# Triangle's two layer norms: variances of four chunks side by side, scale spread by a second product

## The chip, the core and the metric

The kernel runs on one core of a Trainium2 chip. Its time is the device time of one execution in microseconds (us); the figure compared is the median over repeated runs. A profile is one further execution, recorded instruction by instruction. The engines named below are PE (TensorE, matrix products into PSUM), DVE (VectorE), ACT (ScalarE), POOL (GpSimd) and SP (SyncE, which here only issues DMAs). "PEld" is PE loading a stationary operand.

## The reference

Four layers work one after another on an image of 256 by 256 pixels with 128 channels, each preceded by a group norm and added to its input: attention, a gated recurrence, a triangle multiplication and a convolution. The change touches the third. Its core:

```python
def layer_norm(x, w, b):
    mu = jnp.mean(x, axis=-1, keepdims=True)
    var = jnp.var(x, axis=-1, keepdims=True)
    return (x - mu) * jax.lax.rsqrt(var + EPS) * w + b

pair_norm = layer_norm(pair, ln_in_w, ln_in_b)           # first norm
p = jnp.einsum('bijd,hd->bijh', pair_norm, p_in_w)
g = jax.nn.sigmoid(jnp.einsum('bijd,hd->bijh', pair_norm, g_in_w))
left  = g[..., :H] * p[..., :H]
right = g[..., H:] * p[..., H:]
out = jnp.einsum('bikd,bjkd->bijd', left, right / jnp.float32(L))
out = layer_norm(out, ln_out_w, ln_out_b)                # second norm
out = jnp.einsum('bijh,dh->bijd', out, p_out_w)
gate = jax.nn.sigmoid(jnp.einsum('bijd,ed->bije', pair_norm, g_out_w))
return gate * out
```

Both norms run over the 128 channels, which lie on the 128 partitions. So mean and variance of a pixel are sums over partitions, and the kernel forms them with matrix products.

## The kernel before

`triangle` works on the image as [128 channels, 65536 pixels] in three stages. All PE, ACT and DVE instructions of the first and third stage are pinned: each engine runs them in the order in which the code issues them.

**Stage 1, the first norm** (L999 to L1034) walks over 64 blocks of 1024 pixels, two of them to a DMA of 1 MB. For one block, `centre` multiplies the input by a centring matrix `lc` (two products of 512 columns into the PSUM tile `zc`) and ACT squares it into `sq`. `normalise` multiplies `sq` by `omat`, a 128 by 128 matrix of 1/128, so that every partition of `var` holds the variance of its pixel; ACT makes `rs` from it by Ln and Exp, DVE multiplies `zc` by `rs` and then applies the norm's weight and bias, both on DVE. `centre` of block b+1 is issued ahead of `normalise` of block b. `zc` has three PSUM buffers of two banks, `var` one. After each second block POOL's queue writes `zn` to DRAM (`znT`).

**Stage 2** (L1036 to L1068) reads `znT` four times and forms the gated products and the sum over k. It is not touched.

**Stage 3** (L1074 to L1160) walks over 32 pairs of blocks. In the order of PE's products for pair p: `var` (from `sq` of p, four products), `pe` (output gate, four), `zc` of pair p+1 (four), `py` (output product, four). ACT makes `rs` twice, loads the sigmoid table, makes `ga` from `pe` twice, squares `zc` twice and loads the table for Ln and Exp again. DVE multiplies `zc` by `rs` into `on`, then gates, adds the residual and collects statistics. `zc` has two PSUM buffers; `var`, `pe` and `py` share two more under the tag "z". Three loads of 1 MB and one store of 1 MB go with each pair.

A PSUM tile's buffer is given to the next tile of the same tag when every reader of the old tile is done. The stage that matters here is therefore set by three things: the in-order queues of PE, ACT and DVE, the number of buffers of a tag, and what reads a tile last.

A float32 product of 128 by 512 shows up as two LDWEIGHTS and two MATMUL records. In the attention stage (L306 to L350) the same kind of norm is done for the first layer: there DVE copies the centred tile to SBUF as `zs` (L318 to L324), POOL applies weight and bias (L336), and a small product `pbias` (L338) puts four chunks side by side in the array.

Of the kernel before, what the change touches and what calls it, by code (L numbers as in the profile page):

```python
# [17 lines left out]
P = 128  # L18
# [12 lines left out]
class Kernel:  # L31
# [21 lines left out]
    def act(self, out, in_, func, bias=0.0, scale=1.0, **kw):  # L53
        return self.nc.scalar.activation(out, in_, func, bias=bias, scale=scale, **kw)  # L54
# [4 lines left out]
    def mm(self, out, lhsT, rhs, start=True, stop=True):  # L59
        return self.nc.tensor.matmul(out, lhsT, rhs, start=start, stop=stop)  # L60
# [898 lines left out]
    def triangle(self, x2T, x3T, znT, prodD, stats2, shift2, stats3, prepare):  # L959
# [3 lines left out]
        nc, tc, I = self.nc, self.tc, self.i  # L963
        V = nc.vector
        NB, G, CQ = NPIX // 1024, 4, P // 4
        pin = lambda f: lambda *a, **k: tc.keep_in_program_order(f(*a, **k))  # L966
        mm, act, copy = pin(self.mm), pin(self.act), pin(nc.scalar.copy)
        tt, ts, stt, bn = pin(V.tensor_tensor), pin(V.tensor_scalar), pin(V.scalar_tensor_tensor), pin(V.bn_stats)
        table = pin(nc.scalar.preload_act_table_set)
        flat = lambda t: t.rearrange("p k n -> p (k n)")  # L970
        MUL, ADD = ALU.mult, ALU.add
        with ExitStack() as c:
# [17 lines left out]
                        V.tensor_copy(wf[:, :, 2 * n + side, :],  # L990
                                      wpg[m][:, side * P:(side + 1) * P].rearrange("c (g d) -> c g d", g=G))

            zs = c.enter_context(ExitStack())
            zp = zs.enter_context(self.pool(name="tz", bufs=5))


            with ExitStack() as c1:
                io = c1.enter_context(self.pool(name="t1", bufs=3))
                work = c1.enter_context(self.pool(name="t1w", bufs=2))  # L999
                ps = c1.enter_context(self.pool(name="t1s", bufs=3, space=PSUM))  # L1000
                xin, zn, zc, sq = {}, {}, {}, {}

                def centre(b):
                    if b >= NB:
                        return
                    if b % 2 == 0:
                        xin[b // 2] = io.tile([P, 2048], F32, name="xin")
                        nc.sync.dma_start(xin[b // 2], x2T[:, b * 1024:(b + 2) * 1024])
                        zn[b // 2] = io.tile([P, 2048], F32, name="zn")
                    zc[b] = ps.tile([P, 2, 512], F32, name="zc")  # L1010
                    for k in range(2):
                        s = (b % 2) * 1024 + k * 512
                        mm(zc[b][:, k], lc, xin[b // 2][:, s:s + 512])
                    sq[b] = work.tile([P, 1024], F32, name="sq")
                    act(sq[b], flat(zc[b]), AF.Square, bias=cb)

                def normalise(b):
                    var = ps.tile([P, 2, 512], F32, name="var", bufs=1)
                    for k in range(2):
                        mm(var[:, k], self.omat, sq[b][:, k * 512:(k + 1) * 512])  # L1020
                    rs = work.tile([P, 1024], F32, name="rs")
                    act(rs, flat(var), AF.Ln, bias=self.eps)
                    act(rs, rs, AF.Exp, scale=-0.5)
                    z = zn[b // 2][:, (b % 2) * 1024:(b % 2 + 1) * 1024]
                    stt(z, flat(zc[b]), cb, rs, ADD, MUL)
                    ts(z, z, lnw, lnb, MUL, ADD)
                    if b % 2 == 1:
                        nc.gpsimd.dma_start(znT[:, (b - 1) * 1024:(b + 1) * 1024], zn[b // 2])

                table(LN_EXP)  # L1030
                centre(0)
                for b in range(NB):
                    centre(b + 1)
                    normalise(b)  # L1034

            with ExitStack() as c1:  # L1036

# [29 lines left out]
                        nc.gpsimd.dma_start(prodD[g * CQ + d].rearrange("(p a j) -> p a j", p=P, a=2),  # L1067
                                            o.rearrange("p a j b -> p a (j b)"))  # L1068

            zs.close()  # L1070
            prepare(W["kt"], W["wd"], W["bv"])


            with ExitStack() as c1:  # L1074
                io = c1.enter_context(self.pool(name="t3", bufs=3))
                work = c1.enter_context(self.pool(name="t3w", bufs=3))
                ps = c1.enter_context(self.pool(name="t3s", bufs=2, space=PSUM))
                D = [{} for _ in range(NB // 2)]

                def product(wt, src, h, name, **kw):  # L1080
                    z = ps.tile([P, 2, 512], F32, name=name, **kw)
                    for k in range(2):
                        mm(z[:, k], wt, src[:, h * 1024 + k * 512:h * 1024 + (k + 1) * 512])
                    return flat(z)

                def load(p):
                    if p < NB // 2:

                        for n, src in (("zn", znT), ("pr", prodD), ("xin", x2T)):
                            t = D[p][n] = io.tile([P, 2048], F32, name=n)  # L1090
                            for c0, c1 in ((0, 96), (96, P)) if n == "pr" and p == 0 else ((0, P),):
                                nc.sync.dma_start(t[c0:c1], src[c0:c1, p * 2048:(p + 1) * 2048])

                def centre(p):
                    if p < NB // 2:
                        d = D[p]
                        d["zc"] = [product(self.cmat, d["pr"], h, "zc") for h in range(2)]
                        d["sq"] = []
                        for h in range(2):
                            sq = work.tile([P, 1024], F32, name="sq")  # L1100
                            act(sq, d["zc"][h], AF.Square)
                            d["sq"].append(sq)

                def stats(h):
                    for k in range(2):
                        o = h * 1024 + k * 512
                        bn(stats3[:, 4 * p + 2 * h + k, :], x3[:, o:o + 512])

                def gates(p):
                    pe = [product(we, D[p]["zn"], h, "pe", tag="z") for h in range(2)]  # L1110
# [12 lines left out]
                table(LN_EXP)  # L1123
                for p in range(NB // 2):
                    d = D[p]
                    load(p + 2)
                    on, py, x3 = [], [], io.tile([P, 2048], F32, name="x3")
                    hs = [slice(h * 1024, (h + 1) * 1024) for h in range(2)]
                    var = [product(self.omat, d["sq"][h], 0, "var", tag="z") for h in range(2)]
                    for h in range(2):  # L1130
                        rs = work.tile([P, 1024], F32, name="rs")
                        act(rs, var[h], AF.Ln, bias=self.eps)
                        act(rs, rs, AF.Exp, scale=-0.5)
                        on.append(work.tile([P, 1024], F32, name="on"))
                        tt(on[h], d["zc"][h], rs, MUL)
                    if p:
                        gates(p)
                    ga = d["ga"]
                    centre(p + 1)
                    if p + 1 < NB // 2:  # L1140
                        table(LN_EXP)
                    py = [product(wo, on[h], 0, "py", tag="z") for h in range(2)]
# [291 lines left out]
```

## Time and profile before

| what | value |
|---|---|
| runs | 5235.69 us median of 3 (5234.29 to 5239.15) |
| profiled execution | 5238.88 us, span 5237.0 us |
| DVE busy over the span | 4091.4 us (78%) |
| ACT busy over the span | 3684.9 us (70%) |
| POOL busy over the span | 344.4 us (7%) |
| stage 1, first `zc` product to first product of stage 2 | 3284.57 to 3525.38 us |
| stage 3, first `pe` product to start of the last store | 4228.02 to 4700.49 us |

The span is the stretch from the first to the last instruction of the profiled execution; its own time is 1.9 us longer. Busy shares over the whole span mix four layers with different limits, so the two stages are read by themselves, from the timeline of their steady part and from busy times in a window. Stage 1 repeats with every pair of blocks, stage 3 with every pair too, and each has 32 of them.

### The profile page before, as it was taken

To read this page: it belongs to the slowest core of one execution; us is meant where nothing else is said; L and a number is where in the kernel's file an instruction comes from. 1 tells how busy PE (TensorE), PEld (TensorE's weight loads), DVE (VectorE), ACT (ScalarE), POOL (GpSimd) and SP (SyncE) were. 2 spreads that over 40 slices of the span, in tenths; PEclk is the share of its full clock that TensorE was granted. 3 is DMA by queue.
4 is the path that set the end of the run, shared out by engine and by line. 5 is a ranking of instruction groups with operands and counts; after the bars stand their busy time and mean duration, and the time that the engine had idled before them with its cause. 6 is when DMAs were issued, how large, how long until landed. Compare 5 with 4: busy or idle time off the path is not lost.

```text
span 5237.0 us, 75959 instructions
## 1 busy us (share of the span) xinstructions
PE 4997.8 (95%) x30067; PEld 2805.6 (54%) x30067; DVE 4091.4 (78%) x4886; ACT 3684.9 (70%) x5051; POOL 344.4 (7%) x552
## 2 busy tenths in 40 slices
PE   6699999999999899999999998999999989989999
PEld 4433555555555333333333333349999944339999
DVE  5665999999999799999999999554433446679886
ACT  4376888888888799999999998883333357762110
POOL 1132000000000000000000000000011000000000
PEclk7799999999999899999999999999999999999999
DMA  8875222222222122122222221767766678855432
GB/s 290 335 271 206 73 86 82 85 80 83 86 85 82 62 70 70 66 73 68 70 70 67 73 70 65 286 253 272 251 229 231 224 288 295 295 206 188 148 123 65
DMA packets 185921, 788.58 MB, mean 151 GB/s; under 512 B 36083, under 2 KB 39432, under 8 KB 136384
## 3 DMA queue, kind: packets, MB, share of 16 engines
q1 hardware_dynamic: 120212, 514.73, 29.2%
q0 software_dynamic: 60416, 268.46, 13.3%
q8 instruction: 240, 3.93, 0.3%
q10 hardware_dynamic: 4936, 0.50, 0.1%
q14 instruction: 117, 0.96, 0.1%
HBM read 512.28 MB, written 271.32 MB: 150 GB/s over the span
## 4 chain that ended last, share of the span: by engine, by line
issue 50%; PE 41%; DVE 5%; POOL 2%; DMA 1%; ACT 1%; POOLq 0%; ACTq 0%; DVEq 0%; SPq 0%
PE z L60 9%; PE m L60 7%; PE zc L60 4%; PE po L60 4%; PE nd L60 3%; PE sc L60 3%; PE var L60 2%; PE py L60 2%; DVE stats L966 1%; DVE x L966 1%; PE ppq L60 1%; PE ppv L60 1%; PE px L60 1%; PE ppk L60 1%; PE ppg L60 1%
## 5 line engine op out<-in xcount | busy, mean ns | idle before, releaser
L471 DVE TENSOR_TENSOR e<-sc,bT 128x1024 f32<-128x1024 f32 x512 | 602.9, 1219 | 52.0 <-PE sc L60 52.0
L54 ACT ACTIVATE e<-e 128x1024 f32<-128x1024 f32 x512 | 540.3, 1055 | 64.1 <-DVE e L471 54.9
L966 DVE TENSOR_TENSOR LR<-z,sg 128x512 f32<-128x512 f32 x256 | 268.3, 1049 | 365.6 <-ACT sg L54 358.6
L60 PE MATMUL m<-U,v 128*128 128x128 f32 x4608 | 516.6, 276 | 6.6 <-DVE v L1281 6.6
L60 PEld LDWEIGHTS m<-U,v 128*128 128x128 f32 x4608 | 516.4, 192 | 6.7 <-DVE v L1281 6.7
L60 PE MATMUL z<-wf,zt 128*128 128x128 f32 x4096 | 460.9, 276 | 4.3 <-DVE zn L966 3.6
L60 PEld LDWEIGHTS z<-wf,zt 128*128 128x128 f32 x4096 | 460.6, 193 | 5.5 <-DVE zn L966 4.4
L54 ACT ACTIVATE sg<-z 128x512 f32<-128x512 f32 x256 | 152.8, 597 | 308.7 <-PE z L60 306.8
L60 PE MATMUL var<-sq,omat 128*128 128x512 f32 x768 | 360.8, 599 | 1.2 <-ACT rs L54 1.2
L54 ACT ACTIVATE rs<-var,eps 128x1024 f32<-128x1024 f32 x192 | 213.2, 1111 | 169.7 <-PE var L60 169.7
L60 PE MATMUL sc<-tq,tk 32*128 32x256 f32 x4096 | 299.0, 403 | 2.3 <-DVE e L471 1.4
L471 DVE TENSOR_TENSOR ks<-e 128x1024 f32<-128x1024 f32 x256 | 300.6, 1215 | 0.0
L60 PEld LDWEIGHTS sc<-tq,tk 32*128 32x128 f32 x4096 | 187.6, 185 | 160.3 <-issue 97.1
L60 PE MATMUL nd<-e,tv 128*32 128x256 f32 x4096 | 271.8, 383 | 0.0
L60 PE MATMUL zc<-xin,lc 128*128 128x512 f32 x512 | 248.6, 609 | 6.0 <-DVE zn L966 5.5
L54 ACT ACTIVATE dn<-dn 128x512 f32<-128x512 f32 x384 | 241.6, 629 | 12.7 <-DVE dn L471 1.9
L60 PEld LDWEIGHTS var<-sq,omat 128*128 128x128 f32 x768 | 137.9, 189 | 203.8 <-issue 155.2
L60 PE MATMUL av<-y,ident 128*128 128x512 f32 x384 | 192.2, 609 | 44.0 <-DVE y L803 44.0
L60 PE MATMUL po<-LR 128*128 128x256 f32 x1024 | 222.2, 380 | 6.9 <-DVE LR L966 6.9
L1318 ACT COPY m4s<-m 128x512 f32<-128x512 f32 x32 | 18.7, 585 | 286.8 <-PE m L60 286.8
L60 PEld LDWEIGHTS po<-LR 128*128 128x128 f32 x1024 | 194.1, 190 | 34.2 <-DVE LR L966 7.7
L54 ACT ACTIVATE rs<-rs 128x1024 f32<-128x1024 f32 x192 | 202.9, 1057 | 6.1
(325 smaller groups left out, 10085.5 us busy)
## 6 DMA issues: line engine op xcount, KB each, us to landing
zt<-znT SPq DMA_DIRECT2D x128, 1024.0 KB
znT<-zn POOLq DMA_DIRECT2D x64, 1024.0 KB, 4.7
xin<-x2T SPq DMA_DIRECT2D x64, 1024.0 KB
xr<-x3T SPq DMA_DIRECT2D x46, 768.0 KB
xin<-in_x_dram SPq DMA_DIRECT2D x64, 512.0 KB
xT<-xo POOLq DMA_DIRECT2D x64, 512.0 KB, 10.5
xr<-xT SPq DMA_DIRECT2D x64, 512.0 KB
xin<-xT SPq DMA_DIRECT2D x32, 1024.0 KB
```

What stands on the lines that cost most here:

```text
L54: return self.nc.scalar.activation(out, in_, func, bias=bias, scale=scale, **kw)
L60: return self.nc.tensor.matmul(out, lhsT, rhs, start=start, stop=stop)
L471: pin = lambda f: lambda *a, **k: tc.keep_in_program_order(f(*a, **k))
L966: pin = lambda f: lambda *a, **k: tc.keep_in_program_order(f(*a, **k))
L1318: nc.scalar.copy(m4, m[4])
```

## The change

For a pair of blocks there are now four chunks of 512 pixels. A product with `m32`, a [128, 32] matrix of 1/128, gives the variance of one chunk on 32 partitions; four such products write the four quarters of one [128, 512] tile `var`. Ln and Exp then run once over [128, 512] for the pair, in place of twice over [128, 1024]. A second product, with `spread` (all 1/32) over the 32 partitions of a chunk, spreads the scale to 128 partitions: `pr`, two PSUM tiles of [128, 1024]. Since `pr` lies in PSUM, the centred tile is first copied to SBUF as `zs`: by DVE in stage 1 (which adds the bias `cb` on the way), by ACT in stage 3. DVE multiplies `zs` by `pr`. In stage 1, weight and bias are applied by POOL.

All [128, 1024] PSUM tiles of a stage now share one tag, "w", with three buffers of two banks; `var` has the tag "r" with two buffers of one bank.

```diff
+            m32 = wp.tile([P, 32], F32, name="tmean")
+            V.memset(m32, 1.0 / P)
+            spread = wp.tile([P, P], F32, name="tspread")
+            V.memset(spread, 1.0 / 32)
+
+            def variance(ps, work, sq):
+                var = ps.tile([P, 512], F32, name="var", tag="r", bufs=2)
+                for k in range(4):
+                    mm(var[32 * k:32 * k + 32], m32, sq[k // 2][:, (k % 2) * 512:(k % 2 + 1) * 512])
+                rs = work.tile([P, 512], F32, name="rs")
+                act(rs, var, AF.Ln, bias=self.eps)
+                act(rs, rs, AF.Exp, scale=-0.5)
+                return rs
+
+            def spreads(ps, rs):
+                pr = [ps.tile([P, 1024], F32, name="pr", tag="w") for _ in range(2)]
+                for k in range(4):
+                    mm(pr[k // 2][:, (k % 2) * 512:(k % 2 + 1) * 512], spread[32 * k:32 * k + 32], rs[32 * k:32 * k + 32])
+                return pr
...
-                work = c1.enter_context(self.pool(name="t1w", bufs=2))
+                work = c1.enter_context(self.pool(name="t1w", bufs=4))
...
-                    act(sq[b], flat(zc[b]), AF.Square, bias=cb)
+                    act(sq[m, b], zc, AF.Square, bias=cb)
+                    zs[m, b] = work.tile([P, 1024], F32, name="zs")
+                    add(zs[m, b], zc, cb)
...
-                centre(0)
-                for b in range(NB):
-                    centre(b + 1)
-                    normalise(b)
+                for m in range(2):
+                    load(m)
+                centre(0, 0)
+                centre(0, 1)
+                for m in range(NB // 2):
+                    load(m + 2)
+                    centre(m + 1, 0)
+                    rs = variance(ps, work, [sq[m, b] for b in range(2)])
+                    centre(m + 1, 1)
+                    pr = spreads(ps, rs)
+                    zn = io.tile([P, 2048], F32, name="zn")
+                    for b in range(2):
+                        z = zn[:, b * 1024:(b + 1) * 1024]
+                        tt(z, zs[m, b], pr[b], MUL)
+                        nc.gpsimd.tensor_scalar(z, z, lnw, lnb, MUL, ADD)
+                    nc.gpsimd.dma_start(znT[:, m * 2048:(m + 1) * 2048], zn)
...
-                ps = c1.enter_context(self.pool(name="t3s", bufs=2, space=PSUM))
+                ps = c1.enter_context(self.pool(name="t3s", bufs=3, space=PSUM))
...
-                        d["zc"] = [product(self.cmat, d["pr"], h, "zc") for h in range(2)]
-                        d["sq"] = []
+                        d["zs"], d["sq"] = [], []
                         for h in range(2):
+                            zc = product(self.cmat, d["pr"], h, "zc")
                             sq = work.tile([P, 1024], F32, name="sq")
-                            act(sq, d["zc"][h], AF.Square)
+                            act(sq, zc, AF.Square)
                             d["sq"].append(sq)
+                            z = work.tile([P, 1024], F32, name="zs")
+                            act(z, zc, AF.Copy)
+                            d["zs"].append(z)
...
-                    var = [product(self.omat, d["sq"][h], 0, "var", tag="z") for h in range(2)]
-                    for h in range(2):
-                        rs = work.tile([P, 1024], F32, name="rs")
-                        act(rs, var[h], AF.Ln, bias=self.eps)
-                        act(rs, rs, AF.Exp, scale=-0.5)
-                        on.append(work.tile([P, 1024], F32, name="on"))
-                        tt(on[h], d["zc"][h], rs, MUL)
+                    rs = variance(ps, work, d["sq"])
                     if p:
                         gates(p)
+                    pr = spreads(ps, rs)
+                    for h in range(2):
+                        on.append(work.tile([P, 1024], F32, name="on"))
+                        tt(on[h], d["zs"][h], pr[h], MUL)
```

The order of PE's products is then, for a pair in stage 1: `zc` (first half of the next pair), `var`, `zc` (second half), `pr`. In stage 3: `var`, `pe`, `pr`, `zc` of the next pair, `py`.

More of the change, by code (lines that the diff above doesn't have):

```diff
@@ L968, in triangle @@
         tt, ts, stt, bn = pin(V.tensor_tensor), pin(V.tensor_scalar), pin(V.scalar_tensor_tensor), pin(V.bn_stats)
-        table = pin(nc.scalar.preload_act_table_set)
+        table, add = pin(nc.scalar.preload_act_table_set), pin(V.tensor_scalar_add)
         flat = lambda t: t.rearrange("p k n -> p (k n)")
@@ L991, in triangle @@
                                       wpg[m][:, side * P:(side + 1) * P].rearrange("c (g d) -> c g d", g=G))
-            zs = c.enter_context(ExitStack())
-            zp = zs.enter_context(self.pool(name="tz", bufs=5))
+            quarters = c.enter_context(ExitStack())
+            zp = quarters.enter_context(self.pool(name="tz", bufs=5))
+            m32 = wp.tile([P, 32], F32, name="tmean")
+            V.memset(m32, 1.0 / P)
+            spread = wp.tile([P, P], F32, name="tspread")
+            V.memset(spread, 1.0 / 32)
@@ L997, in triangle @@
             with ExitStack() as c1:
                 io = c1.enter_context(self.pool(name="t1", bufs=3))
-                work = c1.enter_context(self.pool(name="t1w", bufs=2))
+                work = c1.enter_context(self.pool(name="t1w", bufs=4))
                 ps = c1.enter_context(self.pool(name="t1s", bufs=3, space=PSUM))
-                xin, zn, zc, sq = {}, {}, {}, {}
-                def centre(b):
-                    if b >= NB:
-                        return
[L1006 to L1010, printed above, removed]
-                    for k in range(2):
-                        s = (b % 2) * 1024 + k * 512
-                        mm(zc[b][:, k], lc, xin[b // 2][:, s:s + 512])
-                    sq[b] = work.tile([P, 1024], F32, name="sq")
-                    act(sq[b], flat(zc[b]), AF.Square, bias=cb)
@@ L1017, in normalise @@
[L1017 to L1020, printed above, removed]
-                    rs = work.tile([P, 1024], F32, name="rs")
-                    act(rs, flat(var), AF.Ln, bias=self.eps)
-                    act(rs, rs, AF.Exp, scale=-0.5)
[L1024 to L1028, printed above, removed]
@@ L1030, in triangle, with load, centre @@
-                table(LN_EXP)
-                centre(0)
-                for b in range(NB):
-                    centre(b + 1)
-                    normalise(b)
+                xin, sq, zs = {}, {}, {}
+                def load(m):
+                    if m < NB // 2:
+                        xin[m] = io.tile([P, 2048], F32, name="xin")
+                        nc.sync.dma_start(xin[m], x2T[:, m * 2048:(m + 1) * 2048])
+                def centre(m, b):
+                    if m >= NB // 2:
+                        return
+                    zc = ps.tile([P, 1024], F32, name="zc", tag="w")
+                    for k in range(2):
+                        s = b * 1024 + k * 512
+                        mm(zc[:, k * 512:(k + 1) * 512], lc, xin[m][:, s:s + 512])
+                    sq[m, b] = work.tile([P, 1024], F32, name="sq")
+                    act(sq[m, b], zc, AF.Square, bias=cb)
+                    zs[m, b] = work.tile([P, 1024], F32, name="zs")
+                    add(zs[m, b], zc, cb)
@@ L1068, in triangle @@
                                             o.rearrange("p a j b -> p a (j b)"))
-            zs.close()
+            quarters.close()
             prepare(W["kt"], W["wd"], W["bv"])
@@ L1076, in triangle, with product @@
                 work = c1.enter_context(self.pool(name="t3w", bufs=3))
-                ps = c1.enter_context(self.pool(name="t3s", bufs=2, space=PSUM))
+                ps = c1.enter_context(self.pool(name="t3s", bufs=3, space=PSUM))
                 D = [{} for _ in range(NB // 2)]
-                def product(wt, src, h, name, **kw):
-                    z = ps.tile([P, 2, 512], F32, name=name, **kw)
+                def product(wt, src, h, name):
+                    z = ps.tile([P, 2, 512], F32, name=name, tag="w")
                     for k in range(2):
@@ L1109, in gates @@
                 def gates(p):
-                    pe = [product(we, D[p]["zn"], h, "pe", tag="z") for h in range(2)]
+                    pe = [product(we, D[p]["zn"], h, "pe") for h in range(2)]
                     if p:
@@ L1128, in triangle @@
                     hs = [slice(h * 1024, (h + 1) * 1024) for h in range(2)]
-                    var = [product(self.omat, d["sq"][h], 0, "var", tag="z") for h in range(2)]
-                    for h in range(2):
-                        rs = work.tile([P, 1024], F32, name="rs")
-                        act(rs, var[h], AF.Ln, bias=self.eps)
-                        act(rs, rs, AF.Exp, scale=-0.5)
-                        on.append(work.tile([P, 1024], F32, name="on"))
-                        tt(on[h], d["zc"][h], rs, MUL)
+                    rs = variance(ps, work, d["sq"])
                     if p:
                         gates(p)
+                    pr = spreads(ps, rs)
+                    for h in range(2):
+                        on.append(work.tile([P, 1024], F32, name="on"))
+                        tt(on[h], d["zs"][h], pr[h], MUL)
                     ga = d["ga"]
@@ L1141, in triangle @@
                         table(LN_EXP)
-                    py = [product(wo, on[h], 0, "py", tag="z") for h in range(2)]
+                    py = [product(wo, on[h], 0, "py") for h in range(2)]
                     last = p + 1 == NB // 2
```

## The prediction

> **What bounds the kernel now.** The page comes first, then the busy times of the two stages in a window of their steady part.
>
> ```profile
> PE 4997.8 (95%) x30067; PEld 2805.6 (54%) x30067; DVE 4091.4 (78%) x4886; ACT 3684.9 (70%) x5051; POOL 344.4 (7%) x552
> ...
> 3302.80:3507.56 204.76, 199.84 (x448) 80.40 (x448) 117.33 (x113) 179.59 (x169) 14.92 (x28) 1.00 0.80 309
> 4267.00:4683.13 416.13, 411.37 (x929) 166.50 (x929) 277.89 (x292) 309.55 (x290) 15.44 (x29) 1.00 0.80 288
> ```
>
> The columns of the last two are window, length, then PE, PEld, DVE, ACT and POOL busy, granted clock, DMA share and GB/s. PE fills both stages (98% and 99%), at full clock; DVE, ACT and the DMA have room. Next, the timelines: one pair of stage 1, then one of stage 3.
>
> ```profile
> 3383.25 1.98 PE L60 MATMUL zc<-xin,lc 128*128 128x512 f32 x4 [0.18 <-DVE zn L966]
> ...
> 3385.07 1.88 PE L60 MATMUL var<-sq,omat 128*128 128x512 f32 x4
> ...
> 3386.78 1.88 PE L60 MATMUL zc<-xin,lc 128*128 128x512 f32 x4
> ...
> 3388.50 1.88 PE L60 MATMUL var<-sq,omat 128*128 128x512 f32 x4
> ...
> 3389.22 1.28 DVE L966 SCALAR_TENSOR_TENSOR zn<-zc,cb,rs 128x1024 f32<-128x1024 f32 x1 [1.75 <-ACT rs L54]
> ...
> 3390.56 1.98 PE L60 MATMUL zc<-xin,lc 128*128 128x512 f32 x4 [0.18 <-DVE zn L966]
> ```
>
> ```profile
> 4396.06 3.66 PE L60 MATMUL var<-sq,omat 128*128 128x512 f32 x8
> ...
> 4399.56 3.73 PE L60 MATMUL pe<-zn,w2e 128*128 128x512 f32 x8
> ...
> 4403.45 3.70 PE L60 MATMUL zc<-pr,cmat 128*128 128x512 f32 x8 [0.16 <-DVE on L966]
> 4406.98 3.60 PE L60 MATMUL py<-on,two 128*128 128x512 f32 x8
> ...
> 4410.42 3.66 PE L60 MATMUL var<-sq,omat 128*128 128x512 f32 x8
> ```
>
> A group of four records (one [128, 1024] tile) takes 1.72 us start to start (3386.78 to 3388.50), so 0.43 a record. A pair of stage 1 takes 3390.56 - 3383.25 = 7.31 us, of which 4 x 1.72 = 6.88 is products; the rest is `zc` waiting for the DVE pass that frees the buffer of three tiles earlier. A pair of stage 3 takes 14.36 us, 8 x 1.72 = 13.76 of it products. What is saved on PE counts here, until a buffer or another engine ends later.
>
> **What the skill says, and this trace.** The Trainium skill's "TensorE: Matmul & The Clock Gate", Part 3, says that products on different 32-row or 32-column strips run at once; "TensorEngine Tiling (Array Packing)", Key Properties, that a change of tiling mode drains the array. The trace has both shapes of the change: `pbias` (128 rows, 32 columns, 512 wide), and `sc` (32 rows, 128 columns, 256 wide).
>
> ```profile
> 403.79 1.88 PE L60 MATMUL zc<-xin,lc 128*128 128x512 f32 x4
> 405.60 1.06 PE L60 MATMUL pbias<-zn,wb 128*32 128x512 f32 x8
> 406.59 1.98 PE L60 MATMUL var<-sq,omat 128*128 128x512 f32 x4
> 408.41 0.59 PE L60 MATMUL zc<-xin,lc 128*128 128x512 f32 x1
> ```
>
> ```profile
> 1005.36 0.61 PE L60 MATMUL nd<-ks,ones 128*32 128x256 f32 x8
> 1005.91 1.15 PE L60 MATMUL sc<-tq,tk 32*128 32x256 f32 x16
> 1006.99 1.12 PE L60 MATMUL ppq<-zn,wq 128*128 128x512 f32 x2
> 1007.95 1.02 PE L60 MATMUL ppk<-zn,rawk 128*128 128x512 f32 x2
> ```
>
> `pbias` has eight records and takes 0.99 us where eight in a row would take 3.44: four side by side. Between the two `zc` lie 4.62 us; less two full groups of 1.72, `pbias` costs 1.18 with its two switches. `sc`: sixteen records of half width in 1.08 us, or four sets of 0.215 and 0.22 of switching; the first full group after it is 0.10 longer (0.96 against 0.86). With 0.09 for the switch into it (403.79 to 405.60 is 1.81, not 1.72), a spread of two sets of 0.43 costs 0.86 + 0.09 + 0.22 + 0.10 = 1.27 us.
>
> "PSUM — Partial Sum Buffer", section on bank collisions, says that two engines must not read one bank at once. The attention norm has the very pair of readers that the change brings to stage 1:
>
> ```profile
> 234.21 1.11 ACT L54 ACTIVATE sq<-zc,cb 128x1024 f32<-128x1024 f32 x1 [1.76 <-PE zc L60]
> ...
> 235.35 1.28 DVE L299 TENSOR_SCALAR zs<-zc,cb 128x1024 f32<-128x1024 f32 x1 [1.53 <-ACT sq L54]
> ```
>
> `zs` doesn't use `sq`, and DVE was idle, yet it starts 0.03 us after the square's end. So the two readers come one after the other, and a `zc` buffer is held for both.
>
> **Stage 1, part by part.** PE: the two `var` groups (3.44 us) go, 1.18 and 1.27 come: 3.44 + 2.45 = 5.89 us a pair. ACT loses four passes of 1.06 to 1.11 and gains two of half width (0.63, the row dn<-dn, and 0.68 as 1.11 - 0.43): 3.5 us. DVE had 117.33 / 28 = 4.19 us a pair; now two copies of 1.28 and two products of 1.22 (the attention norm's rows): 5.0. POOL gets two passes of 1.19 (attention's row zn<-zn,lns,lnb) ahead of each store, 2.9 with the 0.53 of the store; only the last store has a waiter: stage 2's first DVE product (6.99 us at 3533.16), and by the dates below it is issued at about 3525.6, not later than the 3526.47 of before. None of these is the bound. The buffers are.
>
> Tag "w" has three. In PE's order the tiles are Z0, Z1 (the halves of `zc`), pr0, pr1, so Z0 of the next round takes the buffer of Z1, with only the spread between them. From the first record of Z0 at 0: `var` starts at 0.10 (first group after a switch or stall) + 1.72 + 0.09 = 1.91, Z1 0.99 later at 2.90. A tile is read 2.02 us after such a start (3383.25 to the square at 3385.27): 4.92. Square 1.11, hand-over 0.04, copy 1.28, hand-over to PE 0.06 (DVE's end at 3390.50 to 3390.56): the next Z0 can start at **7.41 us**. The spread ends at 4.81 + 1.08 = 5.89 and PE then idles 1.5 us. The other waits end before they are needed: Ln and Exp at 4.4 (spread at 4.81); pr1's buffer, held by Z0, at 4.45; pr0's earlier; DVE's products run from 0 to 2.4 of the next round.
>
> So a pair takes 7.41 where it took 7.31. Over 29 rounds of steady state that is +2.9 us. At the start, Z0 of pair 2 comes at about 3297.0 by the same chain, where its `zc` came at 3299.03: -2.0. At the end, from the last Z0 to stage 2 is 12.2 us (Z1 2.9, read 2.0, square 1.1, `var` 1.1, Ln and Exp 1.3, spread 1.3, two products 2.4) in place of 14.28 (3511.10 to 3525.38): -2.1. **Stage 1: -1 us**, within -5 and +5 for 0.15 us either way in the chain. PE's saving of about 1 us a pair is lost to the buffer.
>
> **Stage 3.** PE: the two `var` groups go: 6 x 1.72 + 1.18 + 1.27 = 12.77 us. Buffers, from `var` at 0: `pe` halves at 1.00 and 2.82. `var` is read at 1.10 (last set at 0.47, 0.63 later); Ln to 1.78, Exp to 2.45, table 1.28 to 3.74, `ga` to 4.78 and, as the second `pe` is ready at 4.74, to 5.76. The spread could start at 4.63; its second half has the buffer of the first `pe`: 4.84. It issues until 5.89; `zc` needs the buffer of the second `pe`, free at 5.82. Then `zc` at 5.89 and 7.71, `py` at 9.43 and 11.15, next `var` at 0.09 + 12.87 = **12.96 us**. Second half of `zc` waits for on0 (spread read at 5.98, product 1.22: 7.2), the first `py` for on1 (8.4), the second for the ACT copy of Z0 (7.91 + two passes of 1.02: 9.9): all in time. The new copies cost ACT two passes (1.01, the row ar<-za), under cover: ACT ends with its table at 13.0, and Ln comes at 14.06. DVE's work is unchanged; the second `py` is read at 13.07, and 1.28 + 2.35 + 2.46 of gate, sums and statistics (4410.69 to 4416.62 in the trace) end at 19.0, just when the next spread is read (18.94), with 0.3 us to spare for `zc`. That is the thinnest cover: what it overruns, it adds to the pair.
>
> DMA: four transfers, 4.19 MB a pair, need 324 GB/s at 12.96 us. The first 30 us of the stage show 348 to 420 GB/s in windows of 10 us, so this fits; the loads are issued two pairs ahead.
>
> The second `var` came at 4252.60; by the same chain it comes at about 4251.3. Thirty rounds of 12.96 in place of 14.36 put the last at 4640.1 in place of 4683.13, and from there to the end it is 1.4 us shorter (first `py` at 7.2, not 8.66): **stage 3: -44 us**.
>
> **Sum.** -1 - 44 = -45 us on the profiled execution's 5238.9, so 5193 to 5194. The three runs lie around 5235.7, 3 us lower: **5190 us**. The two memsets (under 0.3 us each on DVE, by the row two<-w2o of 0.28) are off the path.
>
> **Rivals.**
> - Stage 1 gains too: were the two readers of `zc` not in series, the chain would be 7.41 - 1.11 - 0.04 = 6.26 us, over 5.89 of PE, and give 32 x 1.15 = 37 us more: 5153. Against it: the two lines above. Chance 0.06.
> - Stage 3 gains half: the near ties (spread against `ga`, `zc` against the second `ga`, DVE's statistics) or the DMA cost another 0.5 to 0.9 us a pair: 5205 to 5222. For it: three waits within 0.3 us. Chance 0.12.
> - No change or slower, by the buffers of "w": where the scheduler hands Z0 the buffer that comes free last, it waits for the product that reads pr1 in place of the copy. Stage 1 then takes 7.41 + 2.44 = 9.85 us a pair, +81; with stage 3's gain: 5271. With the product that reads pr0 it is 8.63, +42: 5231, no change. It turns slower from about 8.9 us a pair. Against it: in stage 1 before, `zc` waits for exactly the tile three back. Chance 0.05 for no change, 0.08 for slower.
> - The products don't run side by side: `var` and spread cost 3.44 each, +2.3 and +2.2 us a pair over my prices. Against the old pairs this is 10.4 and 17.2 at least: 5235 + 98 + 91 = 5424. `pbias` and `sc` speak against it. Chance 0.01.
>
> **How the numbers follow.** The forecast has 0.68, with a range of its own of 5172 to 5205: 0.15 us a pair either way in stage 1 (5 us) and 0.3 in stage 3 (10 us). With the half gain, 0.12, this reaches 5222 and holds 0.80: range 5172 to 5222. A difference under 0.2% (10 us) can't be told from none here. Faster: 0.68 + 0.12 + 0.06 = 0.86; same 0.05; slower 0.08 + 0.01 = 0.09.
>
> **What would show it.** Right: in stage 1 `zc` waits for DVE `zs` once a pair, about 1.5 us, and pairs are 7.4 apart; `zs` starts as the square ends; `var` of eight records and `pr` of eight about 1 us each; in stage 3 pairs of 13.0, with PE nearly full. Wrong: `zs` beside the square; PE waiting for `zn` rather than `zs`; stage 3 above 13.5 with PE waiting for `ga`, `on` or a load; a group of eight records near 3.4 us.

## The result, and the profile after

The changed kernel takes 5197.92 us (median of four runs, 5192.49 to 5201.93) where the kernel before takes 5236.49 us (four runs beside it): a ratio of 0.9922 [0.991, 0.9935]. That is 38.6 us less. The forecast was 5190 us, with a range of 5172 to 5222: the direction and the size held, and the gain was put 6 to 8 us too high. How far the mechanism held is read from the stages.

The profiled execution of after is the fastest of the four, 5192.49 us with a span of 5190.7 us. Its stages beside those of the profiled execution of before, each taken from the first product of one kind to the first of the next (`ppq` is the first of attention after its norm):

| stretch | before, us | after, us | difference | predicted |
|---|---|---|---|---|
| attention's first stage and all before it (code not touched): to first `ppq` | 495.63 | 491.11 | -4.5 | 0 |
| rest of attention, recurrence (not touched): to first `zc` | 2788.94 | 2788.30 | -0.6 | 0 |
| stage 1: first `zc` to first `z` | 240.81 | 238.98 | -1.8 | -1 |
| stage 2: first `z` to first `pe` | 702.64 | 706.07 | +3.4 | 0 |
| stage 3 and the head of the convolution: first `pe` to first `m` | 483.34 | 440.47 | -42.9 | -44 |

The rest differs by 0.2 us. Of the 46.3 us between the two spans, 41.3 lie in the three stages of triangle; 5 lie in code that is the same in both kernels, which is how far two executions differ by themselves.

First the page of after: the busy times of its first part, then two rows of its costliest groups (busy us and mean ns of one, then the idle time ahead of them and what ended it).

```profile
PE 4917.5 (95%) x30579; PEld 2748.2 (53%) x30579; DVE 4111.6 (79%) x4888; ACT 3556.5 (69%) x4987; POOL 421.7 (8%) x616
...
L60 PE MATMUL zc<-xin,lc 128*128 128x512 f32 x512 | 250.0, 612 | 44.2 <-DVE zs L966 43.6
...
L54 ACT ACTIVATE sq<-zc,cb 128x1024 f32<-128x1024 f32 x128 | 141.5, 1105 | 128.1 <-PE zc L60 128.1
```

PE has 80 us less to do, and half of that came off the time. The second line says where the rest stayed: `zc` now waits 43.6 us in all for the DVE copy `zs` that frees its buffer (the third, that the squares wait for `zc` in turn). One pair of stage 1 in the timeline of after (start, duration, engine, operation; in brackets the engine's idle time ahead of it and what ended it):

```profile
3388.60 1.99 PE L60 MATMUL zc<-xin,lc 128*128 128x512 f32 x4 [1.45 <-DVE zs L966]
...
3390.51 1.06 PE L60 MATMUL var<-sq,tmean 128*32 128x512 f32 x8
...
3391.51 1.98 PE L60 MATMUL zc<-xin,lc 128*128 128x512 f32 x4
...
3393.42 1.14 PE L60 MATMUL pr<-rs,tspread 32*128 32x512 f32 x8
...
3393.53 1.11 ACT L54 ACTIVATE sq<-zc,cb 128x1024 f32<-128x1024 f32 x1 [0.54 <-PE zc L60]
3394.68 1.28 DVE L966 TENSOR_SCALAR zs<-zc,cb 128x1024 f32<-128x1024 f32 x1 [1.62 <-ACT sq L54]
...
3396.02 1.98 PE L60 MATMUL zc<-xin,lc 128*128 128x512 f32 x4 [1.45 <-DVE zs L966]
```

Read it from the second `zc` on: it starts at 3391.51, its square at 3393.53, the copy at 3394.68, and the next pair's `zc` at 3396.02, 0.06 us after the copy's end. The copy takes nothing from the square, DVE has been idle for 1.62 us, and yet it starts 0.04 us after the square's end. A pair takes 3396.02 - 3388.60 = 7.42 us. In stage 3 one pair of PE looks like this:

```profile
4391.21 1.06 PE L60 MATMUL var<-sq,tmean 128*32 128x512 f32 x8
...
4392.20 3.70 PE L60 MATMUL pe<-zn,w2e 128*128 128x512 f32 x8
...
4395.84 1.37 PE L60 MATMUL pr<-rs,tspread 32*128 32x512 f32 x8
...
4397.14 3.70 PE L60 MATMUL zc<-pr,cmat 128*128 128x512 f32 x8
...
4400.68 3.60 PE L60 MATMUL py<-on,two 128*128 128x512 f32 x8
...
4404.20 1.06 PE L60 MATMUL var<-sq,tmean 128*32 128x512 f32 x8
```

PE shows no idle gap; a pair takes 12.99 us where it took 14.36. The two small groups take 0.99 and 1.30 us to the next start.

Last, the start of stage 2, in the timeline of before and then of after:

```profile
3525.38 8.18 PE L60 MATMUL z<-wf,zt 128*128 128x128 f32 x48 [3.61 <-DVE zn L966]
3526.47 0.53 POOL L1028 DMA_DIRECT2D znT<-zn  x1 [6.52 <-DVE zn L966]
...
3533.16 1.02 DVE L966 TENSOR_TENSOR LR<-z,sg 128x512 f32<-128x512 f32 x1 [6.99 <-DMA znT<-zn]
```

```profile
3518.40 7.25 PE L60 MATMUL z<-wf,zt 128*128 128x128 f32 x48 [1.37 <-DVE zn L966]
...
3519.19 2.36 POOL L1058 TENSOR_SCALAR zn<-zn,ln2in_w,ln2in_b 128x1024 f32<-128x1024 f32 x2
3521.85 0.58 POOL L1059 DMA_DIRECT2D znT<-zn  x1 [0.30 <-POOL zn L1058]
...
3526.63 2.80 DVE L966 TENSOR_TENSOR LR<-z,sg 128x512 f32<-128x512 f32 x3 [7.16 <-issue]
```

The first DVE product into `LR` (the tile of gated products) waits until the last store of stage 1 has landed, as the line of before says; in after the view names no releaser ("issue"), and the last experiment below tests it. The store is issued 1.09 us after PE starts stage 2 in before, and 3.45 us after it in after, behind two POOL passes of 1.19 us each.

### The profile page after: what moved, and what is told of

It reads as the page before. It is cut to its first block, busy times and chain, and to the rows that moved or that the text cites. A ratio compares the mean times of both kernels' runs of the same rounds, so it can differ in the third digit from the quotient of the medians.

```text
span 5190.7 us, 77032 instructions
## 1 busy us (share of the span) xinstructions
PE 4917.5 (95%) x30579; PEld 2748.2 (53%) x30579; DVE 4111.6 (79%) x4888; ACT 3556.5 (69%) x4987; POOL 421.7 (8%) x616
## 4 chain that ended last, share of the span: by engine, by line
PE 54%; DVE 29%; issue 12%; ACT 2%; POOL 1%; DMA 1%; POOLq 0%; ACTq 0%; SPq 0%; DVEq 0%
PE m L60 7%; PE zc L60 7%; PE nd L60 7%; PE sc L60 5%; PE z L60 4%; PE var L60 3%; DVE tr L806 3%; DVE t L803 3%; DVE y L803 3%; DVE p L803 3%; DVE yf L803 3%; PE ppq L60 3%; PE ppv L60 2%; PE px L60 2%; PE pe L60 2%
## 5 line engine op out<-in xcount | busy, mean ns | idle before, releaser
L60 PE MATMUL zc<-xin,lc 128*128 128x512 f32 x512 | 250.0, 612 | 44.2 <-DVE zs L966 43.6
L54 ACT ACTIVATE sq<-zc,cb 128x1024 f32<-128x1024 f32 x128 | 141.5, 1105 | 128.1 <-PE zc L60 128.1
L60 PEld LDWEIGHTS zc<-xin,lc 128*128 128x128 f32 x512 | 93.5, 192 | 189.4 <-issue 94.4
L60 PE MATMUL bx<-p,ident 128*128 128x512 f32 x384 | 192.3, 610 | 0.0
L54 ACT ACTIVATE o<-po 128x256 f32<-128x256 f32 x256 | 84.2, 381 | 146.7 <-issue 115.9
```

## The experiments

Each kernel is the changed one but for the edit shown. Ratios are against runs of the kernel before on the same chip (medians 5237.09 for the first four, 5235.23 for the next four, 5238.49 for the last two). Two questions: which part of the change brings what, and is it the two readers in series that eat stage 1's saving?

**One part alone.** The first kernel has stage 1 of after with stage 3 of before, the second the reverse.

```diff
-                    rs = variance(ps, work, d["sq"])
+                    var = [product(self.omat, d["sq"][h], 0, "var", tag="z") for h in range(2)]
...
+                        tt(on[h], d["zc"][h], rs, MUL)
...
-                    pr = spreads(ps, rs)
...
-                        tt(on[h], d["zs"][h], pr[h], MUL)
```

> The change in stage 1 alone, stage 3 as before. Theory (a zc buffer is held by two readers in series, in a ring of three, which eats PE's saving): pairs of stage 1 stay at 7.42 us against 7.31, the stage's ends give about 4 us back, the last store comes about 2 us later for stage 2: within 5 us of the kernel before. Rival (stage 1 gives a part of the gain, PE's saving of about 1 us a pair): about -30 us.

Measured: 5239.43 us, 1.0007 [0.9998, 1.0015]; pairs of stage 1 7.42 us. In its profile, the longest of its 13 executions (8 us over their median), stage 1 is 0.7 us shorter than before and stage 2 is 6.8 us longer.

```diff
-                for m in range(NB // 2):
-                    load(m + 2)
-                    centre(m + 1, 0)
-                    rs = variance(ps, work, [sq[m, b] for b in range(2)])
-                    centre(m + 1, 1)
-                    pr = spreads(ps, rs)
...
+                for b in range(NB):
+                    centre(b + 1)
+                    normalise(b)
```

> The change in stage 3 alone, stage 1 as before. Theory: all of the gain, -41 to -45 us; pairs of 13.0 us. Rival (the two stages share it): about -10 to -20 us.

Measured: 5197.46 us, 0.9925 [0.9911, 0.9938]; pairs of 7.31 us in stage 1 and 12.99 in stage 3, which is 42.9 us shorter. Stage 2 takes 702.0 us, as before (702.6). So stage 3 alone brings the whole gain, and of these two it is the new stage 1 behind which stage 2 gets longer.

**Is it the hold of the buffer?** If it is, the same products must run faster as soon as a `zc` buffer has one reader. Here ACT squares the copy in SBUF, and DVE alone reads PSUM; Ln and Exp are issued ahead of the squares.

```diff
-                    act(sq[m, b], zc, AF.Square, bias=cb)
                     zs[m, b] = work.tile([P, 1024], F32, name="zs")
                     add(zs[m, b], zc, cb)
+                def square(m, b):
+                    if m < NB // 2:
+                        sq[m, b] = work.tile([P, 1024], F32, name="sq")
+                        act(sq[m, b], zs[m, b], AF.Square)
...
                     rs = variance(ps, work, [sq[m, b] for b in range(2)])
+                    square(m + 1, 0)
                     centre(m + 1, 1)
+                    square(m + 1, 1)
                     pr = spreads(ps, rs)
```

> Whole change, but in stage 1 only DVE's copy reads the PSUM tile; ACT squares the copy. Theory: the hold of a zc buffer loses the 1.11 + 0.04 us of the square, pairs take 2.90 + 2.02 + 1.28 + 0.06 = 6.26 us in place of 7.42, 37 us less than the whole change: about 5160 us. Rival A (the pair is bound by DVE's four passes, POOL or the DMA, not by the hold): 7.2 to 7.4 us, no change against the whole change. Rival B (PE's mode switches): no shorter than 7.0.

Measured: 5168.98 us, 0.9869 [0.9854, 0.9884], 29 us under after and 9 over what was expected. Pairs take 6.33 us (expected 6.26), with two of 8.4 and 8.3 some 50 us into the stage. Stage 1 is 27.3 us shorter than before, stage 2 only 0.5 longer. The line in PE's timeline that answers to the 1.45 us of after:

```profile
3424.05 1.98 PE L60 MATMUL zc<-xin,lc 128*128 128x512 f32 x4 [0.36 <-DVE zs L966]
```

The wait is still for `zs`, but 1.1 us shorter: the square's length has left the chain.

The next kernel leaves both readers and gives the chain more time instead: the two `zc` come first, then the variance of this pair and the spread of the pair before, which needs two more `zs` buffers.

```diff
-                    zs[m, b] = work.tile([P, 1024], F32, name="zs")
+                    zs[m, b] = work.tile([P, 1024], F32, name="zs", bufs=6)
...
                     centre(m + 1, 0)
-                    rs = variance(ps, work, [sq[m, b] for b in range(2)])
                     centre(m + 1, 1)
-                    pr = spreads(ps, rs)
+                    if m < NB // 2:
+                        rs[m] = variance(ps, work, [sq[m, b] for b in range(2)])
...
+                    pr = spreads(ps, rs[m - 1])
...
-                        tt(z, zs[m, b], pr[b], MUL)
+                        tt(z, zs[m - 1, b], pr[b], MUL)
```

> Whole change with both readers of zc as they are, but in stage 1 the variance products stand behind both halves of zc, next to the spread of the pair before. Theory: from Z1's first product to the next Z0 it is still about 4.4 us, but Z1 starts 1.8 us after Z0 in place of 2.9: pairs of 6.2 to 6.3 us, about 5160 us. Rival A (the passes of DVE, POOL or the DMA bound the pair): 7.2 to 7.4 us, about 5198 us.

Measured: 5170.62 us, 0.9874 [0.9859, 0.9889]; pairs of 6.23 us and again two long ones (9.3 and 8.9). Stage 1 is 31.6 us shorter than before, and stage 2 8.2 us longer, which with the long pairs is why the time stayed some 10 us over what was expected. Two different ways of getting the hold off the chain give the same 27 to 29 us.

The opposite: hold each buffer longer, with a second DVE copy that reads `zc`.

```diff
                     add(zs[m, b], zc, cb)
+                    again = work.tile([P, 1024], F32, name="again", bufs=1)
+                    add(again, zc, cb)
```

> Whole change, with DVE reading each centred tile of stage 1 a second time into a buffer that nobody uses. Theory: the hold of a zc buffer grows by the pass (1.2 to 1.28 us), and the pair with it, one for one: 7.42 + 1.2 = 8.6 to 8.7 us, +37 to +41 us on the whole change, about 5237 us. Rival (the pair is bound by something else and DVE, at 5.0 us of 7.42, has room for 2.5 us more): 7.4 us, no change.

Measured: 5282.86 us (two runs), 1.0088 [1.007, 1.0107]. Pairs take 10.24 us, well over what the longer hold explains. One pair on PE:

```profile
3384.68 1.98 PE L60 MATMUL zc<-xin,lc 128*128 128x512 f32 x4
3386.59 2.10 PE L60 MATMUL pr<-rs,tspread 32*128 32x512 f32 x8
3390.43 3.57 PE L60 MATMUL zc<-xin,lc 128*128 128x512 f32 x4 [1.74 <-issue]
3393.92 1.06 PE L60 MATMUL var<-sq,tmean 128*32 128x512 f32 x8
```

From the second `zc` to the next pair's first it is 3390.43 - 3384.68 = 5.75 us, where after has 4.51: +1.24, as a copy more makes it. But the group of `zc` that then starts takes 3.49 us to the next start (3393.92 - 3390.43), where after takes 1.91. That is the other 1.6 us. The busy times in windows (window, length, PE, PEld, DVE, ACT, POOL busy, granted clock, DMA share, GB/s) name it. First a window of after's stage 1, then three of this kernel: the long one, and the two parts of one pair.

```profile
3290.00:3518.40 228.40, 181.97 (x745) 55.33 (x737) 149.69 (x125) 107.06 (x124) 90.78 (x92) 1.00 0.77 290
...
3400.00:3500.00 100.00, 83.69 (x236) 26.03 (x236) 70.14 (x59) 34.12 (x40) 29.45 (x30) 0.83 0.54 204
...
3390.27:3393.68 3.41, 3.25 (x4) 1.17 (x4) 2.32 (x3) 0.00 (x0) 2.11 (x2) 0.50 0.18 77
3393.68:3400.51 6.83, 5.25 (x21) 1.46 (x20) 4.89 (x5) 3.46 (x4) 0.83 (x2) 1.00 0.73 267
```

The granted clock is 0.83, where after has 1.00 in stage 1, and it is not low throughout: it is at half for one piece of 3.41 us in each pair, in which the four products of the slow `zc` group start, and full for the 6.83 us that follow. So the chain did what was expected, and a cost that nobody had expected came on top: the four products at half clock. PE idles 1.74 us in one piece ahead of them, after a spread that has itself waited. That the longer idle is what lowers the clock is the likely reading; no kernel here changed the idle time and nothing else.

**How tight is stage 3?** One ACT pass of [128, 512] more, ahead of the table load, into a tile that nothing uses.

```diff
                     rs = variance(ps, work, d["sq"])
+                    more = work.tile([P, 512], F32, name="more", bufs=1)
+                    act(more, rs, AF.Exp, scale=-0.5)
```

> Whole change, with one more ACT pass of 0.63 us between Exp and the sigmoid's table in stage 3, whose result nobody uses. Theory (after the change the second gate, by its buffer, frees zc's products within 0.1 us of when PE wants them): 12.99 + 0.55 = 13.5 us a pair, +17 us. Rival (ACT is at some 70% of a pair and off the path): no change.

Measured: 5217.87 us, 0.9961 [0.9946, 0.9977], 20 us over after; pairs of 13.66 us. ACT and the PE group concerned, in the timeline of this kernel:

```profile
4409.31 0.63 ACT L54 ACTIVATE rs<-rs 128x512 f32<-128x512 f32 x1
...
4409.97 0.63 ACT L54 ACTIVATE more<-rs 128x512 f32<-128x512 f32 x1
...
4410.62 1.28 ACT L966 ACT_TABLE_LOAD   x1
...
4411.91 1.94 ACT L54 ACTIVATE ga<-pe 128x1024 f32<-128x1024 f32 x2
4412.08 2.03 PE L60 MATMUL pr<-rs,tspread 32*128 32x512 f32 x8
```

That is 0.67 us a pair over after, where 0.55 was expected. The spread takes 2.03 us in place of 1.37, because its second half wants the buffer that the first `ga` reads (it starts at 4412.99, 0.06 us after that pass ends). In after ACT is busy for 74% of this stage (275 of 373 us in its steady part), yet a pass of 0.63 us costs 0.67 us a pair: the stretch from Ln to the second `ga` has no slack at all.

**Both repairs of stage 1 together.** DVE alone reads `zc`, and the spread comes a pair later (the two edits above in one kernel, lines picked from it).

```diff
-                    act(sq[m, b], zc, AF.Square, bias=cb)
+                        act(sq[m, b], zs[m, b], AF.Square)
...
+                        rs[m] = variance(ps, work, [sq[m, b] for b in range(2)])
+                    square(m + 1, 0)
+                    square(m + 1, 1)
...
+                    pr = spreads(ps, rs[m - 1])
```

> Read once and late variance together in stage 1. Theory: the hold no longer ends last, PE does: 0.10 + 3.44 + 0.09 + 0.99 + 1.08 = 5.7 us a pair, about 16 us less than late variance alone, about 5155 us; the reads of the input, which PE waited for once in the faster stage 1, may take a part back. Rival (DMA, at 2.1 MB a pair, now binds): 6.2 us or more, about 5168 us.

Measured: 5155.55 us, 0.9845 [0.9832, 0.9858], as expected: 80 us under before and about 42 under after, faster than either repair alone. PE in its timeline:

```profile
3396.23 3.70 PE L60 MATMUL zc<-xin,lc 128*128 128x512 f32 x8
3399.86 1.07 PE L60 MATMUL var<-sq,tmean 128*32 128x512 f32 x8
3400.86 1.14 PE L60 MATMUL pr<-rs,tspread 32*128 32x512 f32 x8
3401.93 1.55 PE L60 MATMUL zc<-xin,lc 128*128 128x512 f32 x3
```

A pair takes 5.70 us with no idle time. Four pairs are longer (6.7 to 9.2 us), and the waits of PE put them down to loads of `xin` (7.2 us in all). Stage 1 is 42.8 us shorter than before, stage 2 5.5 longer.

**What are the long pairs?** Either the loads are issued too late, or the DMA has no room. First, four loads ahead in five buffers:

```diff
-                        xin[m] = io.tile([P, 2048], F32, name="xin")
+                        xin[m] = io.tile([P, 2048], F32, name="xin", bufs=5)
...
-                    load(m + 2)
+                    load(m + 4)
```

> The same with the input of stage 1 loaded four pairs ahead in five buffers in place of two ahead in three. Theory: the stall of some 5 us about 50 us into stage 1 (loads queued behind stage 2's early loads on SP) goes, and nothing else changes: 3 to 6 us less than read once and late variance together, about 5150 us. Rival (the stall is bandwidth): the same time.

Measured: 5157.18 us, 0.9842 [0.9829, 0.9856], nothing gained over the one before where 3 to 6 us were expected. In its profile the long pairs do lose less, 4.2 us over 5.70 in all against 9.1, and stage 1 is 4.8 us shorter (193.2 against 198.1); but stage 2 is 2.3 us longer (710.4 against 708.1). Busy times by window:

```profile
3320.00:3330.00 10.00, 10.00 (x44) 3.50 (x40) 8.86 (x8) 5.56 (x7) 5.42 (x6) 1.00 1.01 424
3330.00:3340.00 10.00, 10.00 (x43) 3.65 (x40) 8.36 (x8) 6.43 (x8) 4.80 (x6) 1.00 1.01 428
...
3380.00:3480.00 100.00, 97.14 (x442) 35.26 (x439) 80.06 (x67) 55.20 (x69) 53.32 (x55) 1.00 0.83 313
```

For these stretches the DMA is full, at 424 to 428 GB/s, against 313 later in the stage: deeper loading halved the gap and moved it to 3350, where PE waits once, for 2.4 us. The view puts that wait down to `zn`; a transfer lands 0.10 us before PE loads its next weights, the same as at the load waits of the kernel before, so that it is again a load is likely but not shown. The Trainium skill's "DMA: Bandwidth & Descriptors", section "Bandwidth", has 425 GB/s measured for a load of 16 MB on a single core; this trace comes to the same figure with loads and stores of 1 MB together. Stage 2's loads of `zt` start in that stretch, five of 1 MB. With three of them:

```diff
-            zp = quarters.enter_context(self.pool(name="tz", bufs=5))
+            zp = quarters.enter_context(self.pool(name="tz", bufs=3))
```

> Read once and late variance together, with three buffers for stage 2's input in place of five, so that 3 MB in place of 5 are read ahead during stage 1. If the stall 50 us into stage 1 is bandwidth (425 us of GB/s at a full DMA share were seen there), it shrinks with the bytes: about 3 us of its 10 us less at least, about 5151 us. If it is the order of SP's queue: no change, 5155 us.

Measured: 5156.34 us, 0.9848 [0.9834, 0.9861], the same, which is what was expected if the order of SP's queue were the cause. In its profile (8 us over the median) the long pairs are 8.3 to 10.2 us, and the DMA is still full there (397 to 427 GB/s). That the DMA is full is shown. That it is full because of those early loads is not: taking two of five away didn't shrink the gap. What makes the long pairs stays open between the two.

**Stage 2's start.** If `LR` waits because it lies where the stored tile `zn` lay, `zn` in a place of its own must free it. (From the kernel with three.)

```diff
+            out1 = quarters.enter_context(self.pool(name="t1o", bufs=2))
...
-                    zn = io.tile([P, 2048], F32, name="zn")
+                    zn = out1.tile([P, 2048], F32, name="zn")
```

> The same, and the tile that stage 1 stores lies outside the space that stage 2's LR tile takes over, in two buffers. If stage 2's first DVE product waits for the last store because of that space (8 to 12 us in the trace of the faster versions), the wait shrinks to what frees the rest of the space, and stage 2 starts up some 5 us sooner: about 5146 us. If it waits for another thing: no change against three buffers alone.

Measured: 5184.75 us, 0.9901 [0.9886, 0.9916], 28 us slower than the kernel with three. DVE in its timeline shows why:

```profile
3484.33 2.35 DVE L966 TENSOR_TENSOR zn<-zs,pr 128x1024 f32<-128x1024 f32 x2 [1.84 <-DMA znT<-zn]
```

With two buffers in place of three, `zn` waits for its stores; pairs take 5.7 to 12.2 us. The question itself has an answer: the first product into `LR` comes 4.45 us after PE starts stage 2, in place of 9.4 in the kernel with three and 7.8 in before, and stage 2 is only 1.0 us longer than before, in place of 6.9. It comes 1.7 us after the last store is issued (4.8 in after, 6.7 in before), so it no longer waits for that store to land, and the view names ACT's `sg` as what it waits for. So the wait comes from the shared space. Three buffers in a place of their own weren't tried.

## Why the prediction was nearly right

Step by step:

- *The price of the two small groups* held: 1.18 and 1.27 us were read from two other products of before. Stage 3's own starts give 0.99 and 1.30 to the next start, and the whole pair, 12.99 against a forecast of 12.96, leaves no room for another price.
- *Stage 1, buffer in place of array*: pairs of 7.42 us against 7.41, with the named wait of 1.45 us (forecast 1.5) and the copy starting as the square ends. "PE's saving of about 1 us a pair is lost to the buffer" is shown by the kernels that shorten the hold (6.33) or give it time (6.23): both then run faster with the same products.
- *Stage 3, near ties*: the spread started at 4.63 us from `var`, `zc` at 5.93 and `py` at 9.47, where the forecast had 4.63 with the second half at 4.84, 5.89 and 9.43. None of the ties was overrun. That they are ties is shown by the extra ACT pass, which cost its full length.
- *The rivals*: that stage 1 gains too by two readers at once was refuted by `zs` starting only after the square; the half gain by the 12.99; the wrong buffer handed to `zc` by the pair of 7.42; groups that don't run side by side by their 1 us. Most of the 37 us that the first of them named can be had, but not in this order of products: 29 with one reader of PSUM, 27 with both readers and the variance behind both halves of `zc`.

**The term that was mis-sized: what stage 1 leaves to stage 2.** The forecast put the last store at "not later than the 3526.47 of before" and so charged stage 2 nothing; it is 3.4 us longer. By the date the forecast was right (3521.85), but by luck: this execution reached stage 1 5.2 us earlier, and counted from the first `zc` the store is issued at 242.4 us, against 241.9 in before. Stage 2 starts 7.0 us earlier, so that the store now comes 3.45 us after its start and not 1.09, behind the two POOL passes, which are queued behind the store of the pair before.

Little of that distance comes through as waiting: the first product into `LR` comes 8.2 us after the start of stage 2, against 7.8, because it comes 4.8 us after the store's issue and not 6.7. The granted clock accounts for more. First two windows of before, up to where PE goes on after the wait and behind it; then PE where it goes on in after, and a window behind that:

```profile
3525.38:3534.23 8.85, 8.17 (x48) 7.98 (x48) 1.86 (x3) 1.19 (x2) 0.53 (x1) 0.70 0.46 168
3534.23:3544.00 9.77, 9.77 (x87) 9.77 (x88) 5.94 (x6) 3.52 (x6) 0.00 (x0) 1.00 0.76 279
```

```profile
3527.70 8.48 PE L60 MATMUL z<-wf,zt 128*128 128x128 f32 x59 [2.05 <-DVE LR L966]
...
3529.01:3532.42 3.41, 3.41 (x18) 3.41 (x17) 1.47 (x2) 0.60 (x1) 0.00 (x0) 0.50 0.34 70
```

In before the low clock falls on the products ahead of the wait, which hides it; in after the clock is at half for 3.41 us behind the wait, where PE no longer waits, and an estimate of its cost is half of it, 1.7 us. With the 0.45 us by which `LR` comes later this makes 2.15, and the first quarter of stage 2, up to its first product of the sum over k, is 2.07 us longer. The same sum (how much later PE goes on, and half the time at half clock behind it) fits the other kernels within 0.2 us, but for the last two: 6.8 us with stage 1 alone (measured 6.7), 8.4 with the later variance (8.3), 5.5 with both repairs (5.3), and 0.1 with one reader (0.1), where PE had waited 3.34 us and the clock stayed full. With stage 1 of before it is -0.6 (-0.6). The kernel with three `zt` buffers (3.2 against 4.0) and the one with `zn` moved, which doesn't wait (-0.9 against -0.3), don't fit. Why the clock falls behind some of these waits and not behind others isn't shown. The other 1.3 us of after lie in the sum over k of the third quarter and are open.

The two halves measured by themselves come to nearly the same total. Stage 1 with its effect on stage 2 was forecast at -1 and is +2.3 us in the medians (5239.43 - 5237.09), with an interval of -1 to +8 that holds no change too; stage 3 was forecast at -44 and is -39.6 (5197.46 - 5237.09), though its own stretch is 42.9 us shorter in both profiles. Single executions of after differ by 9 us, so those last 3 us can't be placed.

## What to carry to other kernels

Where a change takes work off the busiest engine, follow each buffer from the product that fills it to the last reader that frees it: a second reader of the same PSUM tile that starts only as the first ends adds its full length to that loop, and here it ate the whole saving of one stage while the other kept its own. Let one engine read the tile and the others read its copy, or put the variance behind both halves and its spread a round later; with both, stage 1 went from 7.42 to 5.70 us a pair. And a stage that ends sooner only helps if what the next one waits for comes sooner too: measure the end of that wait from the start of the next stage, not by its date, and look at the granted clock behind it.

## What was not expected of the hardware

- In the kernel with a second copy the granted clock of TensorE stood at half for 3.41 us of every 10.24 (0.83 in the mean), and a group of `zc` took 3.49 us in place of 1.91. PE idles there 1.74 us in one piece in every pair; in after it idles 1.45 us in every 7.42, and the clock stays at 1.00. The Trainium skill's "TensorE: Matmul & The Clock Gate", Part 1, lets the clock fall after an idle window of about 3.4 us; the gaps here were shorter, and came back in every pair. Nor does the length of one gap decide: 3.34 us at the start of stage 2, in the kernel where DVE alone reads `zc`, left it at 1.00, and 2.05 us there in after were followed by 3.41 us at half. Where between these cases it begins wasn't measured.
- Loads and stores of one core together reached 424 to 428 GB/s for tens of microseconds (60 us in the kernel with four loads ahead), while PE waited 7.2 us for loads issued two pairs ahead.
- An engine that is 74% busy can have no slack: in stage 3 an ACT pass of 0.63 us cost 0.67 us a pair.
